# Experts in falling order of their token counts, with fewer slots, in a fused two-layer attention and feed-forward kernel

## The chip, the cores and the metric

The kernel runs on one core of a Trainium2 chip. The metric is the device time of one execution in microseconds (us). The engines are TensorE (PE: matrix products; its weight loads are shown apart as PEld), VectorE (DVE), ScalarE (ACT), GpSimd (POOL) and SyncE (SP). In this kernel SP does little but issue transfers; POOL issues the indirect ones (rows chosen by a list of indices).

## The reference, cut to what matters

Four blocks run one after the other on 800 rows (8 sequences of 100) of 512 numbers: an attention, a mixture-of-experts feed-forward block, a second attention, and a feed-forward block with weights rounded to 8-bit integers. The change touches the second:

```python
def _L0_ffn_ref(x, Wg, W1, W2, W3):
    TOP_K = 2
    E = Wg.shape[0]                                   # 8 experts
    scores = jnp.einsum('btd,ed->bte', x, Wg)
    topk_s, topk_i = jax.lax.top_k(scores, TOP_K)
    probs = jax.nn.softmax(topk_s, axis=-1)
    onehot = (topk_i[..., None] == jnp.arange(E)).astype(x.dtype)
    w = jnp.einsum('btk,btke->bte', probs, onehot)
    y = jnp.zeros_like(x)
    for e in range(E):
        h = silu(einsum('btd,hd->bth', x, W1[e])) * einsum('btd,hd->bth', x, W2[e])
        y = y + w[..., e:e + 1] * jnp.einsum('bth,dh->btd', h, W3[e])
    return y
x = x + _L0_ffn_ref(_layernorm(x), ...)
```

Each row goes to two of eight experts, so the experts share 1600 places, 200 on average. An expert's hidden width is 352, its input and output width 512.

## The kernel before, in words

**Slots.** An expert is not computed on all 800 rows. The kernel gives each row a slot number in each of its two experts (`give_slots`), up to CAP = 240 slots an expert, and computes the expert on its 240 slots: a tile of 128 rows and one of 112 (`SLOTS`). Slots that no row takes hold a row that is written to a place nobody reads. If any expert had more than 240 rows, a branch (`tc.If(spills > 0)`, L1018 to L1110) would compute what did not fit, by loops over experts and row tiles. The number that decides it is made at L929 to L931: the largest count (`most`), compared with CAP, as `spilt`. All five engines load `spilt` into a register (L1011) and branch.

**From scores to rows.** `rank_choices` picks the two experts of a row, `mark_places` and `name_tokens` build 0/1 matrices, and `add_tokens` multiplies them on PE into `found`: the row number in every slot. VectorE turns it into whole numbers, `token_of` (L904). POOL then fetches the rows with one indirect transfer for each tile of slots (`gather`, L908): those of expert 0 into `first_rows`, two tiles taken from the pool `fw` that holds weights of a step called fold; those of expert 1 into `second_rows`. Each row brings its normalised values and four numbers more: its two gate values, the rank of its first expert, and its own place.

**Fold.** Beside the routing, PE works on the second attention's query weights: `fold_first`, `fold_turn`, `fold_second` and `fold_third` (L776 to L809) make the tiles `wqf`. `fold_third` is four transposes on PE and a copy by ScalarE. The last two run at L1189 and, between the two row tiles of expert 0, at L1190.

**The expert loop (L1193 to L1281).** For expert e: `gate_and_up` for three blocks of the hidden width (128, 128, 96) multiplies the weights w12, as the stationary operand, with the slots' columns xgT as the moving one (L1200); ScalarE applies silu, VectorE multiplies gate and up into hT. The last block's up half is made in two half-width products side by side, then added. After the second block VectorE rounds a piece of the last block's weights (`quantise_down`, for e below 4), after the first and the third another kind (`quantise_next`). Then `columns_of(e + 1)` transposes the next expert's rows on PE (L1140) and copies them to xgT (L1142, L1144); `choices` makes the gates; the down product (L1261) takes hT as the stationary operand and the 512 columns of w3 as the moving one; ScalarE and VectorE scale the result to y (L1270, L1272), and POOL adds y to the rows in DRAM (`x_acc`, L1273).

**Order and queues.** In this stage PE, VectorE and ScalarE run in the order written (`tc.manual_schedule`, entered at L1178). SP's queue is in order too. The weights of expert e + 2 are loaded by SP in expert e (`load_expert`, L521 to L527: one transfer for w12, three for w3), at addresses fixed when the kernel is built; there are two buffers. Rows of expert e + 2 are gathered at the start of expert e. The first loads of the loop, three `gu` and one `dn` tile, are held back behind the gather of expert 1 (`tc.issue_after`), and each is also tied to VectorE by a one-element memset (L953, L960). A warm-up activation at L1183 makes ScalarE load its silu table before the loop; its output tile is `most`. After the loop, x_acc is read back (L1291) while PE multiplies other weights (`value_weights`, L1302), and the second attention begins with the transposes at L1312 and the products at L1626.

Of the kernel before, what the change touches and what calls it, by code (L numbers as in the profile page):

```python
# [19 lines left out]
P = 128  # L20
# [9 lines left out]
CAP = 240  # L30
SLOTS = [(0, P), (P, CAP - P)]
W = D + 4
# [18 lines left out]
def tile_kernel(  # L51
# [468 lines left out]

    def load_expert(e):  # L521
        a = ew.tile([P, KC, 2 * HE], F32, tag="w12", name=f"w12_{e}")
        nc.sync.dma_start(a, w12[e].rearrange("(c p) h -> p c h", p=P))
        c = ew.tile([P, 3, D], F32, tag="w3", name=f"w3_{e}")
        for m, (m0, mr) in enumerate(HCH):
            last_in[0] = nc.sync.dma_start(c[:mr, m, :], w3[e, ds(m0, mr), :])
        return a, c  # L527
# [26 lines left out]
    for e in range(NE):  # L554
        nc.gpsimd.memset(rank[:, :, e : e + 1], float(NE - e))

    before = gp.tile([P, P], BF16, tag="before", name="before")
# [217 lines left out]

    def fold_first(t_p, *pairs):  # L776
        pa = bank()
        for n, (i, wq_p, kq_p, qr_p) in enumerate(pairs):
            for c in range(CQ // P):
                for j in range(2):  # L780
                    nc.tensor.matmul(
                        pa[ds(R1 * j, R1), ts(n, P)], qr_p[:, j, c, :], kq_p[:, j, c, :],
                        start=(c == 0), stop=(c == CQ // P - 1),
                    )
        nc.scalar.copy(t_p, pa[:, : 2 * P])
        return [(i, wq_p) for i, wq_p, _, _ in pairs], t_p
# [17 lines left out]

    def fold_third(i, f_p):
        pt = bank()
        for c in range(KC):
            nc.tensor.transpose(pt[:, ts(c, P)], f_p[:, ts(c, P)], ident)
        nc.scalar.copy(wqf[:, :, ts(i, P)], pt.rearrange("p (c r) -> p c r", c=KC))  # L809

    begin(6)
# [87 lines left out]
    turned = fw.tile([P, 2 * P], F32, tag="a_p", name="turned3", bufs=1)  # L899
    u4 = fold_first(turned, loaded.pop(0), loaded.pop(0))  # L900
    add_tokens(5, 7)
    token_of = small.tile([P, 2 * NE], I32, tag="token_of", name="token_of")
    with nc.allow_low_precision(reason="a row and its tile add up to whole numbers under 1024"):
# [4 lines left out]
    def gather(e, tiles):  # L908
        got = []
        for i, xg in enumerate(tiles):  # L910
            n = SLOTS[i][1]
            d = nc.gpsimd.indirect_dma_start(
                out=xg, out_offset=None, in_=x_rows,
                in_offset=bass.IndirectOffsetOnAxis(
                    ap=token_of[:n, 2 * e + i : 2 * e + i + 1], axis=0
                ),
            )
            got.append((xg, d.ins))
        return got
# [7 lines left out]
    slots = {0: gather(0, first_rows)}  # L927
    most = small.tile([P, 1], F32, tag="most", name="most")
    nc.vector.tensor_reduce(most, pn[:, :NE], AX.X, ALU.max)  # L929
    spilt = gp.tile([P, 1], I32, tag="spilt", name="spilt")  # L930
    nc.vector.tensor_scalar(spilt, most, float(CAP), None, ALU.is_gt)  # L931
    f3 = fold_second(*u3[1])
# [13 lines left out]
    xT_first = qw.tile([P, KC, 2 * P], F32, tag="wkr", name="xT_first")  # L946

    def load_gate_up(n, pool=None, behind=False):
        w = rows.tile([P, D], F32, tag="xn", name=f"gu{n}") if pool else qin.tile(
            [P, D], F32, tag="gu", name=f"gu{n}", bufs=GB  # L950
        )
        if behind:
            nc.vector.memset(w[0:1, 0:1], 0.0)  # L953
        nc.sync.dma_start(w, wgu[ts(n, P), :])
        return n, w

    def load_down(n, behind=False):
        w = down.tile([P, NI], F32, tag="dn", name=f"dn{n}")
        if behind:
            nc.vector.memset(w[0:1, 0:1], 0.0)  # L960
        nc.sync.dma_start(w, wdn[ts(n, P), :])
        return n, w
# [39 lines left out]
    def slot_tiles(e):  # L1002
        return [
            slot_rows.tile([P, W], F32, tag="row", name=f"xg{e}_{i}", bufs=4)[:n]
            for i, (_, n) in enumerate(SLOTS)
        ]
# [11 lines left out]
    with tc.If(spills > 0, preferred_fallthrough_block=True):  # L1018


        sp, close_sp = open_pool("spill", side="right")
        wts = sp.tile([P, NT, NE], F32, tag="wts", name="wts")
        for k in range(2):
            nc.vector.scalar_tensor_tensor(
                probs[k], slot1[k], 0.0, probs[k], ALU.is_equal, ALU.mult
            )
            nc.vector.tensor_tensor(
                hots[k], hots[k], probs[k].unsqueeze(2).to_broadcast([P, NT, NE]), ALU.mult
            )
# [80 lines left out]
        close_sp()  # L1110

    close_gp()
    down, close_down = open_pool("down_in", bufs=2, side="right")
# [4 lines left out]
    def choices(e, got):  # L1118
        gates = []
        for i, (xg, _) in enumerate(got):  # L1120
            n = SLOTS[i][1]
            one = ffw.tile([P, 1], F32, tag="one", name=f"one{e}_{i}", bufs=4)[:n]
            nc.vector.tensor_scalar(one, xg[:, D + 2 : D + 3], float(NE - e), None, ALU.is_equal)  # L1123
            gate = ffw.tile([P, 1], F32, tag="gate", name=f"gate{e}_{i}", bufs=4)[:n]
            nc.vector.scalar_tensor_tensor(
                gate, xg[:, D : D + 1], one, xg[:, D + 1 : D + 2], ALU.mult, ALU.add
            )
            place = small.tile([P, 1], I32, tag="place", name=f"place{e}_{i}")[:n]
            nc.vector.tensor_copy(place, xg[:, D + 3 :])
            gates.append((gate, place))  # L1130
        return gates

    def columns_of(e, got, between=lambda: None):
        xgT = ffw.tile([P, KC, CAP], F32, tag="xgT", name=f"xgT{e}")
        for i, (s0, n) in enumerate(SLOTS):
            if i:
                between()
            pt = bank().rearrange("p (c q) -> p c q", c=KC)
# [14 lines left out]
    def load_wo(*heads):  # L1153
# [23 lines left out]

    in_order = tc.manual_schedule(  # L1178
        engines={mybir.EngineType.PE, mybir.EngineType.DVE, mybir.EngineType.Activation}
    )  # L1180
    in_order.__enter__()

    nc.scalar.activation(most, ln_eps, AF.Silu)  # L1183
# [3 lines left out]
    gate_up_in = [load_gate_up(gate_up_left.pop(0), behind=True) for _ in range(GB)]  # L1187
    down_in = [load_down(0, behind=True)]
    fold_third(*folded[0])  # L1189
    turned = columns_of(0, slots[0], lambda: fold_third(*folded[1]))  # L1190
    gates = choices(0, slots[0])

    for e in range(NE):  # L1193
        w12_e, w3_e = experts.pop(e)
        xgT = turned
        hT = ffw.tile([P, 3, CAP], F32, tag="hT", name=f"hT{e}")

        def products(po, cols, c0=0, c1=KC):
            for c in range(c0, c1):
                nc.tensor.matmul(  # L1200
                    po, w12_e[:, c, cols], xgT[:, c, :], start=(c == c0), stop=(c == c1 - 1)
                )

        def gate_and_up(m):
            m0, mr = HCH[m]
            pw = bank()
            s = ffw.tile([P, CAP], F32, tag="silu", name="silu")
            if m < 2:
                products(pw[:, :CAP], ds(m0, P))
                products(pw[:, ds(CAP, CAP)], ds(UP[m], P))  # L1210
                nc.scalar.activation(s, pw[:, :CAP], AF.Silu)
                nc.vector.tensor_tensor(hT[:, m, :], s, pw[:, ds(CAP, CAP)], ALU.mult)
                return
            products(pw[:, :CAP], ds(m0, P))
            for half in range(2):
                products(
                    pw[ds(64 * half, 64), ds(CAP, CAP)], ds(UP64, 64), 2 * half, 2 * half + 2
                )
            nc.scalar.activation(s[:mr], pw[:mr, :CAP], AF.Silu)
            nc.vector.tensor_tensor(hT[64:mr, m, :], s[64:mr], pw[mr:, :CAP], ALU.mult)  # L1220
            up = ffw.tile([64, CAP], F32, tag="up", name="up", bufs=1)
            nc.vector.tensor_copy(up, pw[:64, ds(CAP, CAP)])
            nc.vector.tensor_tensor(up, up, pw[64:, ds(CAP, CAP)], ALU.add)
            nc.vector.tensor_tensor(hT[:64, m, :], s[:64], up, ALU.mult)

# [32 lines left out]
        for m, i in steps:  # L1258
            mr = HCH[m][1]
            s0, n = SLOTS[i]  # L1260
            nc.tensor.matmul(  # L1261
                py[i][:n], hT[:mr, m, ds(s0, n)], w3_e[:mr, m, :],
                start=(m == blocks[0]), stop=(m == blocks[2]),
            )
        for i in range(HC):
            gate, place = gates[i]
            n = SLOTS[i][1]
            y = rows.tile([P, D], F32, tag="xn", name=f"y{e}_{i}")[:n]
# [806 lines left out]
```

## Time and profile before

| | |
|---|---|
| three runs | 620.16, 618.49, 620.06 us; median 620.06 us |
| the profiled execution | 620.09 us, of which the span from first to last instruction is 618.3 us |
| granted PE clock | 0.995 of full speed |
| PE busy | 598.5 us (97% of the span) |
| PEld, DVE, ACT, POOL busy | 398.9, 405.7, 229.4, 240.5 us |
| gate and up products, L1200 | 384 records, 74.1 us |
| down products, L1261 | 96 records, 42.6 us |
| expert stage | 139.4 to 260.5 us |

A number of the form L1200 is a line of the kernel before. A float32 product leaves two records on PE, one for each of two passes. A record's own length (366 ns for 240 columns) overlaps the next; what counts in a stream is the distance from one to the next, which is the length of a merged row divided by its records. Where a row shows an idle time, it stands in square brackets with what ended it, so `[1.49 <-DVE one L1123]` is an idle of 1.49 us. The table by stage shows an engine as busy time (x records), and at the end of the line PE's granted clock, the busy share of the transfer engines (above 1 where transfers overlap) and GB/s.

### The profile page before, as it was taken

To read this page: it belongs to the slowest core of one execution; us is meant where nothing else is said; L and a number is where in the kernel's file an instruction comes from. 1 tells how busy PE (TensorE), PEld (TensorE's weight loads), DVE (VectorE), ACT (ScalarE), POOL (GpSimd) and SP (SyncE) were. 2 spreads that over 40 slices of the span, in tenths; PEclk is the share of its full clock that TensorE was granted. 3 is DMA by queue.
4 is the path that set the end of the run, shared out by engine and by line. 5 is a ranking of instruction groups with operands and counts; after the bars stand their busy time and mean duration, and the time that the engine had idled before them with its cause. 6 is when DMAs were issued, how large, how long until landed. Compare 5 with 4: busy or idle time off the path is not lost.

```text
span 618.3 us, 12464 instructions
## 1 busy us (share of the span) xinstructions
PE 598.5 (97%) x4690; PEld 398.9 (65%) x4690; DVE 405.7 (66%) x1047; ACT 229.4 (37%) x530; POOL 240.5 (39%) x245
## 2 busy tenths in 40 slices
PE   8999999989999999999999999999999999999994
PEld 5767755647777777658876777777777544444442
DVE  4865678746777654253327888889874366776687
ACT  3554445551111111242336555556553121222130
POOL 2131231011333332207963878788685001222020
PEclk9999899999999999999999999999999999999999
DMA  8910086559999989673623242433210401110211
GB/s 282 308 41 32 3 289 183 185 169 292 303 316 289 290 255 284 176 193 105 187 65 95 68 109 68 129 82 95 70 43 2 140 10 32 29 27 10 54 41 68
DMA packets 92935, 83.78 MB, mean 135 GB/s; under 512 B 41196, under 2 KB 69568, under 8 KB 92744
## 3 DMA queue, kind: packets, MB, share of 16 engines
q1 hardware_dynamic: 88775, 73.57, 40.7%
q0 software_dynamic: 4096, 9.38, 6.8%
q8 instruction: 38, 0.62, 0.4%
q14 instruction: 26, 0.20, 0.1%
HBM read 63.75 MB, written 12.36 MB: 123 GB/s over the span
## 4 chain that ended last, share of the span: by engine, by line
PE 71%; DVE 4%; issue 1%; ACT 1%; POOL 1%; DVEq 0%; another core or an unknown queue 0%; ACTq 0%
PE bank L396 13%; PE bank L1200 12%; PE four L1543 11%; PE bank L1507 9%; PE bank L1626 7%; PE bank L1261 7%; PE bank L1801 3%; PE bank L1302 2%; PE four L1471 2%; PE bank L1140 1%; PE four L1570 1%; POOL hid L1818 1%; PE bank L402 1%; DVE y L1930 1%; PE bank L1502 1%
## 5 line engine op out<-in xcount | busy, mean ns | idle before, releaser
L1527 POOL TENSOR_SCALAR e<-e,rs 128x361 f32<-128x361 f32 x96 | 112.9, 1192 | 38.3 <-DVE rs L1523 38.0
L396 PE MATMUL bank<-wvo,ctxT 128*128 128x512 f32 x192 | 84.4, 594 | 0.0
L1200 PE MATMUL bank<-xgT,w 128*128 128x240 f32 (+1 forms) x384 | 74.1, 369 | 1.5 <-DVE one L1123 1.5
L1517 ACT ACTIVATE e<-bank,nm 128x361 f32<-128x361 f32 x100 | 56.6, 567 | 50.1 <-DVE rs L1523 40.8
L1200 PEld LDWEIGHTS bank<-xgT,w 128*128 128x128 f32 (+1 forms) x384 | 64.7, 181 | 12.6 <-issue 6.2
L1543 PEld LDWEIGHTS four<-sq,kv 32*128 32x128 f32 (+1 forms) x1536 | 62.2, 185 | 8.4 <-issue 2.8
L1507 PE MATMUL bank<-kvT,qe 128*128 128x361 f32 x192 | 67.2, 483 | 0.2
L1543 PE MATMUL four<-sq,kv 32*128 32x192 f32 (+1 forms) x1536 | 67.0, 325 | 0.0
L1514 DVE TENSOR_REDUCE nm<-bank 128x1 f32<-128x361 f32 x100 | 50.9, 509 | 23.0 <-PE bank L1507 14.4
L1818 POOL TENSOR_TENSOR hid<-g,u 128x512 f32<-128x512 f32 (+1 forms) x17 | 20.4, 1217 | 111.2 <-ACT g L1809 109.6
L396 PEld LDWEIGHTS bank<-wvo,ctxT 128*128 128x128 f32 x192 | 36.0, 190 | 42.6 <-issue 41.9
L1534 DVE STREAM_TRANSPOSE sq<-e 128x384 f32<-128x384 f32 x96 | 53.7, 559 | 2.1 <-POOL e L1527 1.2
L1273 POOL DMA_INDIRECT x_acc<-y,place x16 | 25.2, 1575 | 74.4 <-ACT y L1272 44.4
L361 POOL TENSOR_TENSOR s<-s,rs 100x800 f32<-100x800 f32 x16 | 24.4, 1522 | 68.4 <-DVE rs L360 36.5
L1507 PEld LDWEIGHTS bank<-kvT,qe 128*128 128x128 f32 x192 | 33.4, 189 | 22.6 <-issue 5.5
L1261 PE MATMUL bank<-w,hT 128*128 128x512 f32 (+3 forms) x96 | 42.6, 593 | 0.0
L1626 PE MATMUL bank<-xT,wqf 128*128 128x256 f32 (+1 forms) x128 | 31.2, 394 | 0.0
L1261 PEld LDWEIGHTS bank<-w,hT 128*128 128x128 f32 (+3 forms) x96 | 17.0, 183 | 19.7 <-issue 15.7
L1801 PE MATMUL bank<-w1q,xqT 128*128 128x512 bf16 (+1 forms) x144 | 29.5, 362 | 0.0
L1626 PEld LDWEIGHTS bank<-xT,wqf 128*128 128x128 f32 x128 | 23.8, 190 | 5.3 <-issue 0.5
L304 PE MATMUL bank<-xnT,wq_sb 128*128 128x200 f32 x128 | 24.6, 353 | 1.6 <-ACT xnT L289 1.4
L1806 DVE SCALAR_TENSOR_TENSOR g<-bank,sx,swb 128x512 f32<-128x512 f32 (+1 forms) x18 | 12.6, 702 | 19.0 <-PE bank L1801 18.4
(299 smaller groups left out, 942.1 us busy)
## 6 DMA issues: line engine op xcount, KB each, us to landing
w<-in_w SPq DMA_DIRECT2D x8, 1408.0 KB
gu<-in_wgu SPq DMA_DIRECT2D x22, 256.0 KB
wq_p<-in_wq SPq DMA_DIRECT2D x8, 512.0 KB
w<-in_w SPq DMA_DIRECT2D x16, 256.0 KB
wo<-in_wo SPq DMA_DIRECT2D x8, 512.0 KB
kq_p<-in_wkcq SPq DMA_DIRECT2D x16, 192.0 KB
kv<-ctx_rot SPq DMA_DIRECT2D x32, 96.0 KB
dn<-in_wdn SPq DMA_DIRECT2D x4, 704.0 KB
```

Of the source, the lines that this page charges most:

```text
L396: nc.tensor.matmul(po[:, :D], lhs[:, c, ds(t * P, r)], rhs[:, c, :], start=(c == 0), stop=(c == chunks - 1),)
L1200: nc.tensor.matmul(po, w12_e[:, c, cols], xgT[:, c, :], start=(c == c0), stop=(c == c1 - 1))
L1261: nc.tensor.matmul(py[i][:n], hT[:mr, m, ds(s0, n)], w3_e[:mr, m, :], start=(m == blocks[0]), stop=(m == blocks[2]),)
L1507: nc.tensor.matmul(ps[:, :L], of_batch(b)[a][:, h, s].rearrange("p g q -> p (g q)"), kvTs[b], start=True, stop=True,)
L1514: nc.vector.tensor_reduce(nm, ps[:, :L], AX.X, ALU.max, negate=True)
L1517: nc.scalar.activation(e[:, :L], ps[:, :L], AF.Exp, bias=nm, accum_out=sm)
L1527: nc.gpsimd.tensor_scalar_mul(e[:, :L], e[:, :L], rs)
L1534: nc.vector.transpose(squares[b, h][:, a * (HT // 2) + s, :], e)
L1543: nc.tensor.matmul(pc[:, g, :cols].rearrange("p (t q) -> p t q", q=32), kv4s[b, j // NBH][ds(32 * g, n), j % NBH, :], eT[ds(32 * g, n), :, ...
L1626: nc.tensor.matmul(pq[:, i, :], wqf[:, c, ts(p0 + i, P)], xT[:, c, :], start=(c == 0), stop=(c == KC - 1),)
L1801: nc.tensor.matmul(pw[:r, :n], xqT[:, c, :r], w1q[:, c, ds(off, n)], start=(c == 0), stop=(c == KC - 1),)
L1818: nc.gpsimd.tensor_tensor(hid[:r, ds(c0, n)], g[:r, :n], u[:r, :n], ALU.mult)
```

## The change

Experts 0 and 1 keep their places and 240 slots. The other six run in falling order of their row counts, found at run time, with 232, 222, 216, 210, 206 and 200 slots. A slot plan for place r in the order is thus fixed, and which expert stands there is data: VectorE sorts the six counts by comparing each with each (`key`, `above`, `behind`, `place_of`), takes the row lists in that order (`token_at`), and makes the experts' numbers (`named`, and `mark` for the gates). SP loads the six numbers into registers, and the weights are loaded at `w12[register]` and `w3[register]`. The spill condition becomes: a count of place r above its slots (`over`).

```diff
-SLOTS = [(0, P), (P, CAP - P)]
+SET = 2
+CAPS = [CAP] * SET + [232, 222, 216, 210, 206, 200]
+def slots_of(e):
+    return [(0, P), (P, CAPS[e] - P)]
+SLOTS = slots_of(0)
...
     def load_expert(e):
+        one = ds(by_load[e] if e >= SET else e, 1)
         a = ew.tile([P, KC, 2 * HE], F32, tag="w12", name=f"w12_{e}")
-        nc.sync.dma_start(a, w12[e].rearrange("(c p) h -> p c h", p=P))
+        nc.sync.dma_start(a, w12[one].rearrange("o (c p) h -> p (o c) h", p=P))
...
+    full_key = gp.tile([P, NE], F32, tag="full_key", name="full_key")
+    for e in range(NE):
+        nc.gpsimd.memset(full_key[:, e : e + 1], float(NE * (CAPS[e] + 1)))
```

The first rows come in another order: the last `add_tokens` runs between the two halves of `fold_first`, and the sort stands around it.

```diff
-    u4 = fold_first(turned, loaded.pop(0), loaded.pop(0))
-    add_tokens(5, 7)
-    token_of = small.tile([P, 2 * NE], I32, tag="token_of", name="token_of")
+    u4 = fold_first(
+        turned, loaded.pop(0), loaded.pop(0), between=lambda: add_tokens(5, 7)
+    )
...
+    nc.vector.scalar_tensor_tensor(key, pn[:, :NE], float(NE), falling, ALU.mult, ALU.add)
+    nc.vector.tensor_tensor(above, by_place(key[:, rest_of]), by_expert(key[:, rest_of]), ALU.is_ge)
...
     slots = {0: gather(0, first_rows)}
-    most = small.tile([P, 1], F32, tag="most", name="most")
-    nc.vector.tensor_reduce(most, pn[:, :NE], AX.X, ALU.max)
+    nc.vector.tensor_reduce(behind[:, rest_of], above, AX.X, ALU.add)
+    nc.vector.tensor_tensor(
+        place_of, by_place(falling[:, rest_of]), by_expert(behind[:, rest_of]), ALU.is_equal
+    )
+    nc.vector.tensor_tensor(moved, place_of, by_expert(key[:, rest_of]), ALU.mult)
+    nc.vector.tensor_reduce(key[:, rest_of], moved, AX.X, ALU.add)
+    nc.vector.tensor_tensor(over, key, full_key, ALU.is_ge)
     spilt = gp.tile([P, 1], I32, tag="spilt", name="spilt")
-    nc.vector.tensor_scalar(spilt, most, float(CAP), None, ALU.is_gt)
+    nc.vector.tensor_reduce(spilt, over, AX.X, ALU.max)
```

Behind the branch, the lists in the new order are made, and the first expert's columns are built differently: `xgT` of expert 0 is a tile of the pool `fw`, both of its row tiles are transposed one after the other, and the two copies to `wqf` (`fold_keep`) stand behind them. `dn` is held back by the order of SP's queue, not by a memset. The six register loads stand behind it.

```diff
+    nc.vector.tensor_tensor(moved, place_of, by_expert(falling[:, rest_of]), ALU.mult)
+    nc.vector.tensor_reduce(mark[:, rest_of], moved, AX.X, ALU.add)
+    nc.vector.tensor_scalar(named[:, rest_of], mark[:, rest_of], -1.0, float(NE), ALU.mult, ALU.add)
+    for v in range(2):
+        nc.vector.tensor_tensor(
+            tokens_at[:, :, v, :], place_of,
+            by_expert(token_of.rearrange("p (e v) -> p e v", v=2)[:, rest_of, v]), ALU.mult,
+        )
+        ...
+        nc.vector.tensor_reduce(
+            token_at[:, 2 * SET :], tokens_at.rearrange("p r v e -> p (r v) e"), AX.X, ALU.add
+        )
...
+    most = small.tile([P, 1], F32, tag="most", name="most", bufs=1)
     nc.scalar.activation(most, ln_eps, AF.Silu)
...
-    down_in = [load_down(0, behind=True)]
-    fold_third(*folded[0])
-    turned = columns_of(0, slots[0], lambda: fold_third(*folded[1]))
+    with tc.issue_after(last_gate_up[0].ins):
+        down_in = [load_down(0)]
+    with tc.issue_after(last_down[0].ins):
+        by_load = {
+            e: nc.values_load(
+                named[0:1, e : e + 1], engines=[mybir.EngineType.SP], min_val=SET, max_val=NE - 1
+            )
+            for e in range(SET, NE)
+        }
+    folded[0] = fold_columns(*folded[0])
+    turned = columns_of(
+        0, slots[0],
+        fw.tile([P, 2, D], F32, tag="wq_p", name="xgT0").rearrange("p j d -> p (j d)")[
+            :, : KC * CAP
+        ].rearrange("p (c q) -> p c q", c=KC),
+    )
+    folded[1] = fold_columns(*folded[1])
+    for one in folded:
+        fold_keep(*one)
```

In the loop CAP becomes the expert's own number, `cap = CAPS[e]`, in products, silu, hT, transposes and row tiles, and the manual order of PE, VectorE and ScalarE is entered before the lists are made, not after the gather of expert 1. Inside the spill branch, the weights of what did not fit follow each expert's own limit.

## The prediction

> **What bounds the kernel now.** I read the page's busy times first (TensorE, PE, 598.5 us of 618.3 us, 97%), then the chain that ended last in order of time, because the change sits in one stage. Between 139.4 us and 260.5 us, the eight experts, the chain names nothing but TensorE:
>
> ```profile
> 154.84 9.07 PE bank L1200 x48
> 163.91 0.97 PE bank L1140 x8
> 164.88 5.17 PE bank L1261 x12
> 170.05 9.07 PE bank L1200 x48
> 179.12 0.97 PE bank L1140 x8
> 180.09 5.17 PE bank L1261 x12
> ```
>
> Columns: start, length, work. Experts 1 and 2 each take 9.07 + 0.97 + 5.17 = 15.21 us: gate and up products, the transposes of the next expert's rows, the down product. Busy time by engine in two such periods (PE, weight loads, DVE, ACT, POOL, then clock, DMA share, GB/s):
>
> ```profile
> 154.60:169.80 15.20, 15.20 (x69) 11.01 (x68) 11.68 (x30) 2.37 (x6) 5.20 (x4) 1.00 1.15 301
> 230.60:245.80 15.20, 15.20 (x69) 11.01 (x68) 6.32 (x19) 2.38 (x6) 3.04 (x2) 1.00 1.00 262
> ```
>
> PE is busy for all of the period; VectorE (DVE) comes next with 11.7 us; the DMA share is about 1, so transfers queue. The start of the stage is not PE bound:
>
> ```profile
> 130.37 0.19 DVE L904 TENSOR_REDUCE token_of<-bank 128x16 int32<-128x32 f32 x1 [1.18 <-PE bank L768]
> 130.93 1.23 POOL L912 DMA_INDIRECT first_rows<-x_rows,token_of  x1 [31.46 <-DVE spilt L931]
> 132.46 0.96 POOL L912 DMA_INDIRECT first_rows<-x_rows,token_of  x1 [0.30 <-PE bank L808]
> 137.36 0.55 PE L1140 MATMUL bank<-ident,first_rows 112*128 112x112 f32 x4
> 138.15 0.59 ACT L1144 COPY xgT<-bank 128x512 f32<-128x512 f32 x1 [0.88 <-PE bank L1140]
> 138.17 0.06 DVE L960 MEMSET dn<- 1x1 f32 x1 [2.23 <-remote]
> 138.67 0.62 DVE L1142 COPY xgT<-bank 128x448 f32<-128x448 f32 x1 [0.44 <-DVE dn L960]
> 139.40 0.85 PE L1200 MATMUL bank<-xgT,w 128*128 128x240 f32 x3 [1.49 <-DVE one L1123]
> ```
>
> VectorE stands behind the memset of dn until 138.17, then behind a row of semaphore waits, and both copies into xgT come late; PE idles 1.49 us.
>
> **Part 1, fewer columns in experts 2 to 7.** The slots go from 240 to 232, 222, 216, 210, 206 and 200, in all 8 + 18 + 24 + 30 + 34 + 40 = 154 columns. The gate and up products stream slots as columns. Of 48 records per expert, 40 use the whole array and 8 are half-width pairs running side by side: 44 turns. Price of a column: in the chain 48 records of 256 columns take 10.44 us (0.2175 each, L1626), 30 of 512 columns 12.88 us (0.429, L1302), so 0.83 ns a column. Does it hold below 240? 200 columns have run:
>
> ```profile
> 25.16 5.68 PE L304 MATMUL bank<-xnT,wq_sb 128*128 128x200 f32 x32
> 25.16 5.37 PEld L304 LDWEIGHTS bank<-xnT,wq_sb 128*128 128x128 f32 x32
> ```
>
> That is (5.68 - 0.33) / 31 = 0.173 us a record; the line through 256 and 512 gives 0.171. The weight loads (128x128, as in L1200) do not set a floor at 200. Saving: 44 x 0.83 ns x 154 = 5.62 us. The second row tile's transposes also shrink: 4 x 0.83 x 154 = 0.51 us. The down product (L1261) streams the 512 weight columns and keeps its 5.17 us. Sum 6.1 us, all on the path, as long as nothing else becomes last.
>
> A rule that speaks against this part: the Trainium skill, "TensorE: Matmul & The Clock Gate", section "Back-to-back issue gap", says that spacing in a stream of load and product pairs is set by both, and gives about 81 ns at 128 columns and 131 at 512. By that slope (0.13 ns a column) the two terms would be 48 x 0.13 x 154 = 1.0 us, an estimate, and the time about 618. The rows L304 and L1626 follow another slope, and the sum goes by them.
>
> What covers it: (a) VectorE in experts 0 to 3. The third block's hT waits behind quantise_down. In expert 2 it is ready at 182.98 and its product starts at 183.38 without an idle. With 222 slots PE loses 12 x 18 + 4 x 24 columns = 0.26 us ahead of that point, six DVE and ACT steps give back about 0.11: slack 0.4 becomes 0.25. If it went, each 0.1 us short costs 0.1 us in three experts. (b) Weights. By the semaphores of the trace, w12 of expert 3 is issued at 163.96 and lands at 171.49, for use at 185.3; w3 lands at 181.6 for 195.3; the rows land at 164.7 for 179.1. The lead is 13 us, and the experts move up by at most 6 us in all.
>
> **Part 2, first rows.** add_tokens(5,7) moves between the two halves of fold_first. It waits for token_in (DVE, until 129.18), not for the second half's load and products (129.20 to 129.97), so token_of comes at about 129.6 rather than 130.37, although key and above (two steps of 0.2 us) now stand ahead of it on VectorE. The two gathers on POOL follow 0.8 us earlier; the second, which landed at 137.26, should land at 136.0 to 136.9. xgT of expert 0 goes into a tile of the fold pool, so its copies lose the row of waits; the memset of dn leaves VectorE; the copies of wqf go behind those of xgT. New chain: f_p6 transposes end at 136.43, first_rows 128 at 136.87, first_rows 112 at 137.25 (4 x 0.095 after), copy 137.45 + 0.62 = 138.07, first product 138.1. Gain 1.3 us; bounds 0.4 (second gather lands as late as before) and 1.6.
>
> **Part 3, what is added.** On VectorE six short steps instead of two before spilt (end 131.0 rather than 130.82; the branch reads it at 131 to 132.7, PE last at 132.5), and six more after the branch, 133.9 to 135.15, under the 2.56 us in which VectorE waited for L798 until 135.24: nothing; 0.1 to 0.3 us if each takes 0.25, because f_p6's copy stands behind them. POOL: eight memsets of full_key beside those of rank, before its last softmax products; nothing.
>
> SP: six register loads. One cost 0.47 + 0.24 + 0.15 = 0.86 us at 130.96 (spilt), so 5.2 us, from 138.5 to 143.7; they stand ahead of dn1 (due at 160) and the transpose of gu_q0 (ready at 145.7), in a stretch where SP was idle from 139.1 to 145.7. Six to twelve us is the bound; at twelve w12 of expert 2 goes out 3 us late with 13 in hand. Each of 24 weight loads gets a register operation (0.19 us row of the spilt load) and a run-time address. SP issues for 8.8 us of the 15.2 at most, so 0.8 us more is hidden.
>
> ScalarE: the Silu warm-up no longer stands before the experts; in the built order it is the first thing ACT does (a table load more, under 2.44 us of waiting for the first mv), and a second table load stands directly before the first silu, with that silu's waits, the one on PE among them. Such a load is in the trace:
>
> ```profile
> 525.26 1.28 ACT L1809 ACT_TABLE_LOAD   x1 [7.50 <-DVE g L1806]
> 526.55 1.15 ACT L1809 ACTIVATE g<-g 128x512 f32<-128x512 f32 x2
> ```
>
> It starts when its input is there and costs 1.29 us. In expert 0 silu, hT and quantise move back by 1.29, of which VectorE's idle of 0.87 before the second hT takes most; 0.44 remains, and the ten semaphores that now stand before quantise_down add about 0.1. The third hT, ready at 152.52 with its product at 152.93, comes at 153.05: PE loses 0.2 us (bounds 0 and 0.5). Six more semaphores stand on PE before the first down product, 0.1 us each in this trace, partly under the transposes: 0.2 us.
>
> The Trainium skill, "ScalarE: Activation LUTs", section "What ACT_TABLE_LOAD costs", puts a drain of about 1380 ns on top of each switch. Taken so, expert 0 would lose some 1.4 us more and the sum would be 614.5, an estimate. In the two rows above the ACTIVATE starts 1.29 us after the load, with no further gap.
>
> **Sum**, against the profiled execution: 620.09 us with a span of 618.3, as good as the median of 620.06. 6.1 + 1.3 - 0.2 - 0.2 = 7.0 us less: 613.1 us. After expert 7 everything is placed relative to it (x_acc rows, normalisation, L1312 without idle), and the rest of the kernel is PE bound too, so the gain should arrive at the end whole.
>
> **Rivals.**
> 1. Transfers take over as the bound. For: DMA share 1.0 to 1.15 in six periods. Against: landing times after issue (7.5, 9.1, 8.1, 7.9 us for w12 of experts 3 to 6) do not grow, and PE waits for none. If the period stayed at 15.2 us, only the start's gain would be left: 620.1 - 1.3 + 0.4 = 619.2 us. Partly so, with PE starting to wait when 13 us of lead are gone, 614 to 618.
> 2. The start gives nothing (second gather no earlier, copies behind other waits, VectorE's new steps in front of f_p6): 613.1 + 1.3 = 614.4; with the late hT at its bound 614.9.
> 3. Slower: SP's queue becomes the bound because a load with a run-time address costs far more there. SP has 15.2 - 8.8 = 6.4 us free in the fullest period, about 5.5 in a shorter one; four such loads an expert decide from 1.4 us more each. The nearest rows are POOL's indirect transfers, 0.97 to 1.58 us against 0.38 on SP: up to 1.2 more, just short. At 4 us more each, six experts overrun by 10.5 us, 63 in all, of which the lead takes 13: 613 + 50, about 663.
> 4. The change does not do what it says: an expert exceeds its slots and the spill branch runs, 56 passes with a gather and a scatter of about 6.7 us each in turn, over 700 us more. The counts of experts 2 to 7 worked out from the reference's inputs are, sorted, 223, 211, 208, 190, 189, 167; the slots leave 8 or more free.
>
> **How the numbers follow.** Forecast 0.75, rival 2 0.12, rival 1 0.09, rivals 3 and 4 together 0.04. The predicted time is the forecast's 613.1. Its own bounds: start at best and nothing lost, 612.3; both gains a little larger (0.85 ns a column) and a run as low as the lowest before (618.49, 1.6 us under), 611. Upwards: rival 2 and the lesser part of rival 1, 616.5. What a measurement of this kernel can tell from no change is 0.3%, 1.9 us: faster is under 618.2. Rival 1 whole counts as same, rivals 3 and 4 as slower: 0.91, 0.05, 0.04.
>
> **What would show it.** L1200's line (L1301 after) should fall from 9.07 us an expert to about 7.6 in the last; the sum over eight by 5.6. L1140's (L1228) second half shrinks to 4 x 72 columns. The first L1301 should start near 138.1; the first silu should have a table load of 1.28 us directly before it. Wrong if PE shows idles before L1301 that end on a DMA, if the period stays near 15.2, if SP's issues lie end to end, or if work of lines 1113 to 1170 appears at all.

## The result, and the profile after

The changed kernel takes 625.44 us (median of 6 runs, 622.51 to 627.01) against 619.94 us before (6 runs, 618.49 to 620.24): 1.0084 times the time, interval 1.0063 to 1.0105. The forecast was 613.1 us. So 5.5 us were lost where 7.0 should have come, and the question is what took 12.5 us. The profiled execution, 623.77 us, is the second shortest of the six; what the longer ones lost beyond it was not traced.

Landmarks of three profiled executions, in us from the span's start (the third is the first experiment below, in which two of the six sizes are two slots different):

| | before | after | two sizes moved |
|---|---|---|---|
| execution, span | 620.09, 618.3 | 623.77, 622.0 | 612.27, 610.5 |
| first gate and up product of expert 0 | 139.40 | 137.37 | 137.15 |
| end of expert 7's down product | 260.52 | 262.34 | 252.83 |
| between the two: eight experts | 121.12 | 124.96 | 115.68 |
| first transpose of the second attention | 273.23 | 276.84 | 265.54 |
| from there to PE's last product | 338.2 | 338.6 | 338.4 |

The start came 2.0 us earlier (forecast 1.3; part of it is luck of this pair of executions, see part 2 below), the rest of the kernel is the same, and the loss lies in the expert stage (3.8 us more instead of 6 less) and right behind it (14.5 us instead of 12.7).

The page of after, busy times and the two product lines (busy time, mean ns, idle before and what ended it):

```profile
PE 596.1 (96%) x4690; PEld 395.9 (64%) x4690; DVE 407.3 (65%) x1058; ACT 231.9 (37%) x532; POOL 244.6 (39%) x253
...
L1301 PE MATMUL bank<-xgT,w 128*128 128x240 f32 (+13 forms) x384 | 70.0, 357 | 0.4 <-DVE one L1209 0.4
...
L1362 PE MATMUL bank<-w,hT 128*128 128x512 f32 (+15 forms) x96 | 45.0, 617 | 6.1 <-DVE hT L1325 6.0
```

and the same two lines on the page of before:

```profile
L1200 PE MATMUL bank<-xgT,w 128*128 128x240 f32 (+1 forms) x384 | 74.1, 369 | 1.5 <-DVE one L1123 1.5
...
L1261 PE MATMUL bank<-w,hT 128*128 128x512 f32 (+3 forms) x96 | 42.6, 593 | 0.0
```

L1301 is L1200 of before: 74.1 us became 70.0, so columns were saved; with two sizes moved the line is at 68.5, the 5.6 less that were forecast. L1362 is the down product: it had no idle before, and now PE waits 6.0 us ahead of it, once, for hT. The timeline of after around that wait, in expert 3 (start, length, work, idle before it):

```profile
183.38 3.45 SPq L176 DMA_TRANSPOSE w2q<-dn_q  x1
...
188.11 1.48 POOL L956 DMA_INDIRECT xg<-x_rows,token_at  x1 [0.30 <-issue]
...
192.10 3.63 PE L1362 MATMUL bank<-w,hT 128*128 128x512 f32 x8
...
199.16 0.89 DVE L167 TENSOR_SCALAR dn_q<-dn 128x1408 bf16<-128x1408 f32 x1 [6.43 <-DMA w2q<-dn_q]
...
201.33 0.38 DVE L1325 TENSOR_TENSOR hT<-silu,up 64x222 f32<-64x222 f32 x1
...
201.76 3.78 PE L1362 MATMUL bank<-w,hT 96*128 96x512 f32 x4 [6.03 <-DVE hT L1325]
```

Read it from the bottom: PE waits for the third block of hT; VectorE, which runs in the written order, makes it only at 201.33 because it stood 6.43 us ahead of writing dn_q; dn_q could not be overwritten because the transposing transfer that reads it (w2q<-dn_q), issued at 183.38, landed at 199.06 by its semaphore, 15.7 us later. Before, the four transfers of that kind landed after 5.9 to 9.6 us. The one to compare, here in the timeline of before, landed at 190.88, and VectorE wrote dn_q at 195.57 without a wait:

```profile
181.28 1.43 SPq L167 DMA_TRANSPOSE w2q<-dn_q  x1
```

Two gathers had a part in the delay. At 188.11 POOL issued that of expert 5's second tile: 82 rows. Counted in the packets of the trace, the gather of 128 rows issued just ahead moves its 64 packets within the microsecond from 192 us; those of the 82 rows follow at 4 to 12 a microsecond until 198 us, and meanwhile the transpose's packets of 256 bytes take 177 ns each (median) where 18 ns are usual. The other is the gather of expert 3's 94 rows, issued at 156.35 and landed at 168.75: beside it SP needed 6.55 us to issue the transpose of dn_q at 164.14 (2.51 with two sizes moved), a transpose of gu_q issued at 171.41 landed at 183.31, SP waited 3.6 us for that one, and so the transpose of dn_q went out at 183.38 and not at about 179.4 as with two sizes moved.

The idle then cost the clock. The table by stage of after (PE, weight loads, DVE, ACT, POOL, then clock, DMA share, GB/s):

```profile
185.00:200.00 15.00, 10.73 (x54) 7.68 (x52) 6.24 (x12) 1.66 (x4) 5.65 (x4) 0.94 1.09 215
200.00:215.00 15.00, 13.24 (x52) 10.34 (x52) 8.12 (x25) 1.39 (x3) 6.26 (x4) 0.72 1.09 322
```

The granted clock was at half from 198.1 to 208.3 us. PE worked in 6.6 of those 10.2 us and so lost 3.3. With the idle of 6.0 that is 9.3 us: the eight experts should have taken 124.96 - 9.3 = 115.6, which is what they take in the third column of the table.

The last 1.8 us stem from the same kind of event at the end of the stage. Transfers of after from 236 to 256 us in 40 slices (the share of the 16 transfer engines that is busy, in tenths, and GB/s):

```profile
DMA  9999999004999999999999999999211199111111
GB/s 434 366 417 394 417 286 285 1 11 74 328 393 385 270 262 258 279 308 316 315 348 355 318 381 386 338 309 156 62 33 33 33 33 66 33 26 52 49 49 40
```

and the timeline of after there:

```profile
237.94 2.42 POOL L1374 DMA_INDIRECT x_acc<-y,place  x1 [0.31 <-issue]
...
254.47 0.15 DVE L1218 CAST place<-xg 72x1 int32<-72x1 f32 x1 [7.97 <-DMA x_acc<-y,place]
254.54 0.74 DVE L1371 TENSOR_SCALAR y<-bank,gate 78x512 f32<-78x512 f32 x1
255.18 1.59 POOL L1374 DMA_INDIRECT x_acc<-y,place  x1 [14.82 <-ACT silu L1312]
```

The scatter of expert 5's 82 rows is issued at 237.94 and lands at 254.45. Once the weights have come, one or two tenths of the engines are busy and 33 GB/s flow where 300 to 400 did, which is what two of sixteen engines at work would show. VectorE stands 7.97 us ahead of a one-column cast, because `place` has four buffers and this one still belongs to that scatter; the scatters of experts 6 and 7 go out late behind it, the last at 266.85 instead of 262.51, and PE waits 1.62 us for the first normalised rows.

What marks the two guilty tiles in the packets: counted by size, the packets that POOL issued between 130 and 300 us hold none of 8 bytes before, and 1993 after. They come in bursts: 322 at 160 to 165 us, 667 at 210 to 220, 304 at 190 to 200, 574 at 240 to 250. Now 322 is 14 x 23, 658 (of the 667) is 14 x 47, 280 (of the 304) is 14 x 20 and 574 is 14 x 41, and 47 and 41 are half of 94 and 82 (a packet of a gather holds two rows, so 23 and 20). The other second tiles, of 104, 88, 78 and 72 rows, leave 9 to 40 each, and these too come out as packets of one engine times the engines left out, with 13, 11, 13 and 12 engines at work.

### The profile page after: what moved, and what is told of

Its sections match the earlier page's. It is cut to its first block, busy times and chain, and to the rows that moved or that the text cites. A ratio compares the mean times of both kernels' runs of the same rounds, so it can differ in the third digit from the quotient of the medians.

```text
span 622.0 us, 12552 instructions
## 1 busy us (share of the span) xinstructions
PE 596.1 (96%) x4690; PEld 395.9 (64%) x4690; DVE 407.3 (65%) x1058; ACT 231.9 (37%) x532; POOL 244.6 (39%) x253
## 4 chain that ended last, share of the span: by engine, by line
PE 47%; DVE 5%; DMA 2%; POOL 1%; issue 1%; ACT 1%; ACTq 0%; DVEq 0%; SPq 0%
PE bank L405 13%; PE four L1644 10%; PE bank L1608 9%; PE bank L1727 7%; PE bank L1902 3%; PE four L1572 2%; DMA x_acc<-y,place 2%; PE four L1671 1%; POOL hid L1919 1%; PE bank L411 1%; DVE y L2031 1%; POOL e L1628 1%; PE bank L1413 1%; PE bank L1603 0%; DVE y L2034 0%
## 5 line engine op out<-in xcount | busy, mean ns | idle before, releaser
L1301 PE MATMUL bank<-xgT,w 128*128 128x240 f32 (+13 forms) x384 | 70.0, 357 | 0.4 <-DVE one L1209 0.4
L1301 PEld LDWEIGHTS bank<-xgT,w 128*128 128x128 f32 (+1 forms) x384 | 63.9, 185 | 9.1 <-issue 7.2
L1374 POOL DMA_INDIRECT x_acc<-y,place x16 | 27.5, 1718 | 74.3 <-DVE place L1218 18.8
L1362 PE MATMUL bank<-w,hT 128*128 128x512 f32 (+15 forms) x96 | 45.0, 617 | 6.1 <-DVE hT L1325 6.0
L1362 PEld LDWEIGHTS bank<-w,hT 128*128 128x128 f32 (+15 forms) x96 | 16.5, 180 | 27.8 <-issue 16.6
L1902 PEld LDWEIGHTS <-xqT 128*128 128x128 bf16 x144 | 13.8, 98 | 16.7 <-DMA xqT<-xq 2.1
```

The source lines that it names most:

```text
L1301: nc.tensor.matmul(po, w12_e[:, c, cols], xgT[:, c, :cap], start=(c == c0), stop=(c == c1 - 1))
L1362: nc.tensor.matmul(py[i][:n], hT[:mr, m, ds(s0, n)], w3_e[:mr, m, :], start=(m == blocks[0]), stop=(m == blocks[2]),)
L1374: d = nc.gpsimd.indirect_dma_start(out=x_acc, out_offset=bass.IndirectOffsetOnAxis(ap=place[:, 0:1], axis=0), in_=y, in_offset=None, compu ...
L1902: nc.tensor.matmul(pw[:r, :n], xqT[:, c, :r], w1q[:, c, ds(off, n)], start=(c == 0), stop=(c == KC - 1),)
```

## The experiments

Three theories went in. A: an indirect transfer spreads its rows over as many transfer engines as the largest number up to 16 that divides the row count; 94 = 2 x 47 and 82 = 2 x 41 leave two engines, and whatever else is queued on those two waits. B: the six register loads and the run-time addresses on SP delay the transfers. C: the new steps on VectorE and the late table load delay hT. The Trainium skill, "DMA: Bandwidth & Descriptors", section "Why a DMA increments its semaphore by 16 and not by 1", states the rule of A, with 100 rows on 10 engines and 127 on one as examples. No run here has those counts; the packets counted above, 14 for each one of a working engine with 94 and 82 rows, agree with it.

**e1, two sizes moved by two slots.**

```diff
-CAPS = [CAP] * SET + [232, 222, 216, 210, 206, 200]
+CAPS = [CAP] * SET + [232, 224, 216, 208, 206, 200]
```

> The changed kernel with two of its six sizes moved by two slots: 224 for 222 and 208 for 210, so second tiles of 96 and 80 rows for 94 and 82. Theory A (row counts): an indirect transfer spreads its rows over as many transfer engines as the largest number up to 16 that divides the row count; 94 and 82 leave two of 16, whose 8-byte fillers the trace counts (14 x 47 = 658 and 14 x 41 = 574), and everything queued on those two waits. Then the PE idle of 6.0 us at the third block of expert 3 and the half-clock stretch behind it are gone, no bursts of 8-byte packets over 60 remain, and the time falls to 613 to 616 us. Theory B (the register loads and run-time addresses on SP delay the transfers), theory C (VectorE's new steps and the table load delay the third hT): nothing of that is touched, 624 to 626 us.

Measured: 614.22 us, 0.991 of before (0.9895 to 0.9925). The answers on the transfers of `place` (durations on POOL; landing) for after and for this run:

```profile
L1374 POOL DMA_INDIRECT x_acc<-y,place x16: 1483/1606/2629, 153.1 to 266.9; - x16
...
DMA to landing us min/median/max: 4.6/8.4/16.5
```

```profile
L1374 POOL DMA_INDIRECT x_acc<-y,place x16: 1452/1584/1686, 153.3 to 254.9; - x16
...
DMA to landing us min/median/max: 4.8/7.6/9.3
```

The longest landing falls from 16.5 to 9.3 us, no 6 us wait and no half clock is left in the stage, and the largest burst of 8-byte packets in 5 us is 40. Two slots up in one expert and two down in another are worth 11 us. Registers, addresses, sort and table load are untouched, so B and C fall as the cause of the loss.

**e2, all of the change but the narrow experts.**

```diff
-CAPS = [CAP] * SET + [232, 222, 216, 210, 206, 200]
+CAPS = [CAP] * SET + [CAP] * 6
```

> The changed kernel with all six sizes set to 240: order, sort, register loads, run-time addresses, table load and the new order of the first rows stay, no columns are saved and every second tile has 112 rows. Theory A: the loss is gone with the row counts; what is left is the gain at the start (1.3 us) less the late table load and semaphores (0.4): 619 us, 618 to 620. Theories B and C: the delays stay and no columns are saved: 628 to 632 us.

Measured: 619.21 us, 1.0003 of before (0.9962 to 1.0045). The wide interval says no more than that order, registers and table load cost nothing like 9 us. The stage takes 121.25 us against 121.12 before, so run-time addresses cost nothing that shows in it. Order, sort and addresses were not run one by one.

**e3 and e4, the kernel before with two narrow experts, 222 and 224.**

```diff
+NARROW = {3: 222, 5: 222}          # e4: 224
+def slots_of(e):
+    return [(0, P), (P, NARROW.get(e, CAP) - P)]
...
-            n = SLOTS[i][1]
+            n = slots_of(e)[i][1]
...
+        cap = NARROW.get(e, CAP)
...
-                    po, w12_e[:, c, cols], xgT[:, c, :], start=(c == c0), stop=(c == c1 - 1)
+                    po, w12_e[:, c, cols], xgT[:, c, :cap], start=(c == c0), stop=(c == c1 - 1)
```

> The kernel before with experts 3 and 5 (167 and 211 rows) on 222 slots, at fixed addresses, with no sort and no register: second tiles of 94 rows in two experts, 36 columns fewer. Theory A: both scatters and both gathers of 94 rows go through two transfer engines, bursts of 8-byte packets of about 300 and 650 appear, and the time rises to 622 to 628 us. Theories B and C: only the columns count, 36 x 44 x 0.83 ns = 1.3 us and 0.1 for the transposes: 618.6 us.

> The run before this one with 224 slots for 222: 96 rows for 94, 32 columns fewer than the kernel before. Theories A, B and C alike: 32 x 44 x 0.83 ns = 1.2 us and 0.1 for the transposes less: 618.7 us. The difference of the two runs is theory A's alone.

Measured: 222 slots 631.61 us, 1.0196 of before (1.0123 to 1.0269); 224 slots 619.20 us, 1.000 (0.996 to 1.004). The first is above its expected 622 to 628, in A's direction. Nothing of the change is in these kernels but the row count. The transfers of e3 from 207 to 222 us, while its scatter of 94 rows (issued 206.84, landed 223.04) runs:

```profile
DMA  9999999999999999942999999999999999999999
GB/s 451 373 351 422 394 356 316 297 296 286 295 279 373 419 415 421 186 52 27 190 127 61 46 47 43 46 48 45 45 49 56 46 55 51 48 44 48 48 46 45
```

and of e4, same stretch, 96 rows (issued 204.48, landed 210.71):

```profile
DMA  9999999007999999999999909699999998999999
GB/s 264 231 225 208 221 228 96 11 13 216 198 377 383 451 368 383 428 390 383 421 390 277 200 0 147 126 377 313 352 361 382 371 377 312 324 307 219 213 202 218
```

In e3 the row of nines looks like a full load, and 45 GB/s say that it isn't. Counted in packets from 214 to 222 us, SP's transfers move nothing but the 256-byte packets of transposes, and each takes 172 ns (median) where e4 has 18; a packet counts as busy for all of that time. Beside them the scatter has two packets under way. By what path two engines slow the transposes' packets on all the others was not followed up. PE pays in three ways: 2.4 us of waiting for hT in expert 3, behind dn_q as in after, 3.5 us of waiting for the weights w12 at 237.1 us, and 10.2 us at half clock. The 8-byte packets of e3 number 1960 = 2 x 658 + 2 x 322 (scatters, gathers); e4 has none.

**e5, all second tiles divisible by 16, and e6, the smallest such sizes.**

```diff
-CAPS = [CAP] * SET + [232, 222, 216, 210, 206, 200]
+CAPS = [CAP] * SET + [224, 224, 224, 208, 208, 192]      # e5
+CAPS = [CAP] * SET + [224, 224, 208, 192, 192, 176]      # e6
```

> The changed kernel with sizes 224, 224, 224, 208, 208 and 192 for experts 2 to 7: 160 columns fewer than at 240 (the run with two sizes moved had 156), and every second tile divisible by 16 (96, 96, 96, 80, 80, 64). Theory A, if 13, 11 and 12 engines cost as good as nothing: the same as with two sizes moved, 613.5 to 614.5 us. If they cost something too (A2): 611 to 613 us. No 8-byte packet in the expert stage in either case.

> The changed kernel with the smallest multiples of 16 that hold this draw's counts (223, 211, 208, 190, 189, 167): 224, 224, 208, 192, 192, 176, which is 224 columns fewer than at 240. Against the run with two sizes moved (156 columns, 614.2 us) 68 more: 68 x 48 x 0.83 ns = 2.7 us less, 611.5 us, if columns stay the price. If VectorE or the transfers have become last in the shorter periods (12.5 to 14.2 us each): 613 to 615 us, with PE idles ahead of the third down block.

Measured: e5 617.78 us (612.81 to 623.65), 0.9959 (0.9921 to 0.9998); e6 614.36 us, 0.994 (0.9906 to 0.9975). Both miss: e5 is above either of its answers, and e6 lies in its second range, but without the idles on PE that this range was argued from. Neither has an 8-byte packet in the stage and neither is faster than e1, so no gain from sixteen engines over 13, 11 and 12 shows. Why e5's runs spread over 11 us stays open. e6 should have gained 2.7 us over e1 and did not, without an idle on PE. Its timeline in expert 5, a second tile of 64 rows, has the down product and the weight loads for it (PEld):

```profile
219.98 6.25 PE L1362 MATMUL bank<-w,hT 128*128 128x512 f32 x12
...
221.04 0.19 PEld L1362 LDWEIGHTS bank<-w,hT 128*64 128x64 f32 x2 [0.76 <-ACT xgT L1232]
...
222.04 0.30 PEld L1362 LDWEIGHTS bank<-w,hT 128*128 128x128 f32 x2 [0.81 <-DVE amax L171]
```

The 12 products take 6.2 us, in expert 6 with 64 rows too, and 5.7 in expert 7 with 48 (5.2 to 5.3 in experts 1 to 4). A weight load of 128x64 behind one of 128x128 starts only 0.95 us after it, when the two products ahead are through, and the products stand 0.52 us apart instead of 0.43.

**e7, only the scatters.** In the kernel before, the two scatters of experts 3 and 5 move 94 rows for 112; gathers and columns stay.

```diff
-            n = SLOTS[i][1]
+            n = 94 if i and e in (3, 5) else SLOTS[i][1]
             y = rows.tile([P, D], F32, tag="xn", name=f"y{e}_{i}")[:n]
...
-                out=x_acc, out_offset=bass.IndirectOffsetOnAxis(ap=place[:, 0:1], axis=0),
+                out=x_acc, out_offset=bass.IndirectOffsetOnAxis(ap=place[:n, 0:1], axis=0),
```

> The kernel before, in which only the scatter of the second tile of experts 3 and 5 moves 94 rows for 112; gathers, columns and all else stay (rows 94 to 111 of those tiles stand for no row of x). Theory A: two bursts of 658 8-byte packets, the two scatters land 13 to 17 us after issue instead of 6; without the slow gathers only VectorE's wait for place and y is left: 621 to 627 us. If the slow gathers alone did it: 619 to 620 us. Theories B and C: 619.4 us.

Measured: 623.33 us, 1.0071 (1.0046 to 1.0096); 1316 = 2 x 658 packets of 8 bytes; longest landing 17.2 us against 8.1 before. Slow scatters alone cost some 3.4 us, so the greater part of e3's 12 us comes with the gathers, or with both together.

**e8, one engine.** e3 with 225: 97 rows, a prime number.

```diff
-NARROW = {3: 222, 5: 222}
+NARROW = {3: 225, 5: 225}
```

> The kernel before with experts 3 and 5 on 225 slots: second tiles of 97 rows, a prime number. Theory A: all 97 rows on one transfer engine, 97 x 0.176 us = 17 us for a scatter, against 8.3 us with 94 rows: landing more than 20 us after issue, about 15 x 97 = 1455 fillers of 8 bytes for a scatter, and a time clearly above that of 222 slots (631.6 us): 640 to 665 us. If it were something else about odd or unaligned counts and not the largest divisor: about as with 222 slots, 626 to 635 us.

Measured: 656.78 us, 1.0597 (1.0557 to 1.0637). Its 8-byte packets number 4350 = 2 x 15 x 97 + 2 x 15 x 48; the two scatters land after 28.6 and 31.0 us. Three slots more than 222, and 25 us more: it is the divisor, not the size.

**e9 and e10, tiles of 65 and of 64 rows.**

```diff
-CAPS = [CAP] * SET + [232, 222, 216, 210, 206, 200]
+CAPS = [CAP] * SET + [224, 212, 208, 193, 193, 193]      # e9
+CAPS = [CAP] * SET + [224, 212, 208, 192, 192, 192]      # e10
```

> The changed kernel with sizes 224, 212, 208, 193, 193, 193: second tiles of 96, 84, 80 and three times 65 rows, on 16, 14, 16 and 13 transfer engines; 217 columns fewer than at 240. The tight run (224 columns fewer) showed no idle on PE, but products 0.52 us apart instead of 0.43 wherever a tile of 64 rows or fewer alternates with one of 128. Theory T: the price is of tiles of 64 and fewer rows. Then 65 rows cost nothing: 61 columns more than with two sizes moved, 61 x 48 x 0.83 ns = 2.4 us less than its 614.2: 611.8 us, and the 12 down products of experts 5 and 6 take 5.2 us. If the price comes with any small tile: about 614 us.

> The run before this one with 192 for 193, so tiles of 64 rows in the last three experts, 220 columns fewer than at 240. Theory T: 1.0 us more for the down products and 0.2 for the transposes of each of experts 5 and 6, half of it in expert 7, so about 3 us above the run before: 614.8 us. If the tile of 64 rows costs nothing: 0.1 us below it, 611.7 us.

Measured: 65 rows 610.63 us, 0.9865 (0.9817 to 0.9912), the fastest of all; 64 rows 615.14 us, 0.9913 (0.9887 to 0.9938). One row fewer costs 4.5 us by the medians. The timeline of e9 in expert 5:

```profile
219.63 5.37 PE L1362 MATMUL bank<-w,hT 128*128 128x512 f32 x12
220.11 0.14 PEld L1362 LDWEIGHTS bank<-w,hT 128*65 128x65 f32 x1 [0.24 <-issue]
220.54 0.14 PEld L1362 LDWEIGHTS bank<-w,hT 128*65 128x65 f32 x1 [0.29 <-issue]
```

Now each load lies under the product ahead of it, one every 0.43 us. In e10 the down products of experts 5, 6 and 7 take 6.18, 6.18 and 5.80 us (e9: 5.21, 5.21, 5.32) and the transposes of three tiles 0.97 (0.74): 3.1 us in all, as theory T had it. On top, that execution, the slowest of the five, has a wait of 1.9 us for hT in expert 3, behind the same dn_q, and 3.4 us at half clock after it. The transpose of dn_q landed there 15.4 us after its issue although no tile has fewer than 14 engines by theory A: such a transfer can also come late for another reason, which was not followed up. The Trainium skill, "TensorEngine Tiling (Array Packing)", section "Key Properties", says that a change of tiling mode drains TensorE. That a tile of 64 columns runs in another mode than one of 128 is not shown here; if it does, that fits 0.52 against 0.43 us. What the two runs show is that the step lies between 64 and 65.

**e11, 70 rows.** `CAPS` with 224, 212, 208, 198, 198, 198.

> The changed kernel with sizes 224, 212, 208, 198, 198, 198: the last three second tiles have 70 rows, on 14 transfer engines; 202 columns fewer than at 240. By the columns alone 46 x 48 x 0.83 ns = 1.8 us less than with two sizes moved: 612.4 us, 0.6 above 193.

Measured: 612.10 us, 0.9878 (0.9837 to 0.9918), as expected from the columns.

**e12, four engines.** e3 with 220: 92 rows.

> The kernel before with experts 3 and 5 on 220 slots: tiles of 92 rows, four transfer engines by theory A, 23 rows of 0.176 us = 4.0 us each for a scatter, against 1.2 us with 16 engines and 8.3 with two. 40 columns fewer are worth 1.6 us. Landing times rise by about 3 us. If the stall sets in only when the transfers run over a period: 618 us. If every microsecond of landing counts: 620 to 623 us.

Measured: 620.39 us (618.73 to 624.92), 1.0014 (0.9976 to 1.0053); longest landing 14.5 us. The interval holds both answers, so whether four engines cost time here stays open; they cost far less than two.

## Why the prediction was wrong, point by point

- **The step that failed** is the cover in part 1. The prediction took the new row counts 104, 94, 88, 82, 78 and 72 as columns of products alone. The change also altered 12 indirect transfers, the gather and the scatter of six second tiles, and these were not in the list of what it touches; "the rows land at 164.7 for 179.1", under (b), was carried over as if fewer rows could only land sooner. e3 against e4 shows the term that was missing: +12.4 us for 94 instead of 96 rows in two experts, in a kernel without the change. In after it is 9.3 us in the stage and 1.8 behind it.
- **Rival 1** was the nearest, for the wrong reason. It priced the transfers as a common load, from 614 to 619.2 us. Its argument against, that landing times do not grow, was read from a kernel whose indirect transfers have 128 and 112 rows only, both divisible by 16. It also had PE wait for weights. PE did so in e3 (3.5 us) and e8 (1.7), but not in after: there VectorE waited for a buffer, and everything behind it in the written order waited too; that is how 6.0 us reached PE although weights had 13 us of lead.
- **The clock** had no term. An idle of 6.0 us brought 10.2 us at half clock, worth 3.3 us more.
- **Part 1, the columns**, held. In after, gate and up records stand 0.203 us apart at 240 columns and 0.169 at 200, which is 0.85 ns a column (forecast 0.83). The slope weighed against it, 0.13 ns, does not hold for these float32 products. The line L1301 of e1 is 5.6 us below L1200 of before, as forecast. e1 saves 5.4 us in the stage, and 6.0 with the late hT taken out, for 156 columns priced at 6.2; e9 saves 7.9 for 217 priced at 8.6, 0.5 of the difference being that hT.
- **Part 2, the first rows**, held. The timeline of after:

```profile
129.78 1.23 POOL L956 DMA_INDIRECT first_rows<-x_rows,token_of  x1 [32.40 <-DVE spilt L980]
131.31 0.96 POOL L956 DMA_INDIRECT first_rows<-x_rows,token_of  x1 [0.31 <-POOLq L1067]
...
135.96 0.60 PE L1228 MATMUL bank<-ident,first_rows 112*128 112x112 f32 x4 [0.42 <-DMA first_rows<-x_rows,token_of]
...
136.60 0.62 DVE L1230 COPY xgT<-bank 128x448 f32<-128x448 f32 x1 [2.20 <-PE bank L1228]
...
137.37 5.30 PE L1301 MATMUL bank<-xgT,w 128*128 128x240 f32 x25 [0.37 <-DVE one L1209]
```

  The copy into xgT follows its transposes at once, and the idle of 1.49 us has become 0.37. The first product was forecast for 138.1 and came at 137.37, 2.0 us earlier than before. But the profiled execution of before, like that of e12, ran at half clock for 3.4 us from about 66.5 us, in the first attention, and the two reached the transposes of x_all at 102.7 and 102.9 us, where the others with the old order did at 101.0 to 101.4. Without these two, the four with the old order (e3, e4, e7, e8) have the first product at 138.88 on the mean; the seven with the new order have it at 137.53, without e2, which ran at half clock from 128.8 us. The difference is 1.3 us, as forecast (bounds 0.4 to 1.6). But 0.4 of it stands already at the transposes of x_all (101.2 and 100.8 us on the mean), ahead of what the forecast counted; the new order of the first rows itself is worth 0.9. That the sum came out is in part luck.
- **Part 3** held. The table load stands where it was said, directly ahead of the first silu, in after:

```profile
140.92 1.28 ACT L1312 ACT_TABLE_LOAD   x1 [3.29 <-PE bank L1301]
142.22 0.37 ACT L1312 ACTIVATE silu<-bank 128x240 f32<-128x240 f32 x1
```

  The load starts 0.06 us after the semaphore that it waits for, and silu 1.30 us after the load, so no drain of 1.38 us comes on top here. Expert 0's down product takes 5.25 to 5.78 us instead of 5.17 in the kernels that keep this order: 0.1 to 0.6 us, forecast 0.4 with the semaphores. SP's six register loads take 3.4 us in after, from 136.9 to 140.2 (forecast 5.2), and with the run-time addresses they cost nothing that shows (e2's stage: 121.25 us).
- **Rivals 3 and 4** did not come about: a load of w12 at a run-time address takes SP 0.38 us to issue as before, and no work of the spill branch stands in the trace.
- **The sum.** Without the two sizes, e1 measures 614.22 us, 5.2 less than the 619.43 us before that it was compared with, where the forecast's 7.0 would have been 612.4; its profiled execution was at 612.27. By the medians 1.8 us of the 7.0 are missing, and no trace shows where. So the mechanisms forecast were there, under a loss that the forecast had not looked for. Among the bounds, rival 2's 614.9 counts 0.2 us of the late hT twice; 614.7 would be right, which changes nothing.

## What to carry to other kernels

When a tile's row count changes, price the transfers that carry it as well as the products: look for the largest divisor up to 16 (96, 80, 65 and 70 rows did well here, 94, 82 and 97 did not), and watch GB/s, not the busy share, since packets that crawl or wait count as busy (e3: nine tenths busy at 45 GB/s). One slow transfer is felt where a small buffer is reused on an engine that runs in order, far from the transfer itself. Sizes that merely fit are not the best ones: 224, 212, 208 and three times 193 took 610.63 us, 1.35% less than before (interval 0.9 to 1.8%) and 2.2% less than 232 to 200 (each against before); they leave 0 to 4 slots free for five of these six counts (223, 211, 208, 190, 189, 167), and other inputs would meet the spill branch sooner.

## What the hardware showed that was not expected

- While a scatter of 94 rows ran, all transfers of the core together moved about 45 GB/s (e3), with 97 rows some 33 (e8), against 280 to 450 in the first part of e3's stretch. The packets of 8 bytes, 9 ns long at the median, number as if each engine left out got one for each packet that a working one moves: 14 x 47 (94 rows), 15 x 97 (97 rows), 12 x 23 (92 rows, e12).
- POOL itself needs longer to issue such a scatter: 1.6 us usually, 2.6 with 94 rows, 4.0 with 97.
- Half clock came, up to the kernel's last microseconds, in stretches of 3.4, 6.8, 10.2 and 13.7 us, multiples of 3.41. Idles on PE of 2.4 and 3.5 us (e3), 5.0, 8.4 and 12.7 us (e8), 6.0 us (after) and 1.9 us (e10) ran into or were followed by one; an idle of 1.9 us ahead of the second attention in e7 was not. An idle of 1.4 us that ends at 66.3 to 66.7 us, in all executions with the old order, was followed by one in two of six (before, e12).
- A stationary tile of 64 columns between tiles of 128 costs about 0.17 us at each change of width (1.0 us in 12 products, e6), one of 65 columns nothing (e9).
